# Three taps of VectorE's chains go to ScalarE and GpSimd, and a sampling's last six rounds are kept free

## The chip, the cores and the metric

The kernel runs on one NeuronCore of a Trainium2 chip. The metric is the device time of one execution in microseconds (us); lower is better. The profile names the engines PE (TensorE's matmuls), PEld (its weight loads), DVE (VectorE), ACT (ScalarE), POOL (GpSimd) and SP (the queue that issues most DMAs).

## The reference

Four images of 256 channels, 64x64 pixels, float32, go through four layers. Each is `x = x + layer(groupnorm(x))`.

```python
# layer 0: deformable convolution (DCN) and an MLP
y   = leaky_relu(bn(conv1x1(x)));  t = leaky_relu(bn(depthwise3x3(y)))
offset, mask = conv1x1(t), softmax(conv1x1(t))        # 4 groups x 9 points a pixel
d   = conv1x1(sum_points(mask * bilinear_sample(conv1x1(y), offset)))
x2  = bn(y + d);  x3 = x2 * sigmoid(se_up(relu(se_down(mean(x2)))))
out = y + fc2(leaky_relu(fc1(x3)))
# layer 1: linear attention with a second scale
qkv = relu(bn(conv1x1(x)));  agg = depthwise5x5(qkv) * w + b     # 768 channels, 25 taps
q, k, v = split(concat(qkv, agg));  out = relu(bn(proj((v k^T) relu(q) / sum)))
# layer 2: 3x3 convolution with binarised weights
# layer 3: non-local attention of 4096 positions over the 1024 of a 2x2 max pooling
```

## The kernel before

Channels lie on the 128 partitions, in two halves. The work on an image is written as Python generators that emit instructions and yield a cost after each piece:

- `sample(n)`: the bilinear sampling of image n, 288 rounds. A round (`gathered`) has four indirect DMAs, which GpSimd issues (L607) and which gather 128 rows into one of seven buffers `g`, and small matmuls that weigh and add them (L614). Eighteen rounds are a block; its sums are turned (L619, L624, L634), projected with `ow` (L647), added to y (L653) and stored as x2 (L661).
- `feedforward(n)`: squeeze and excitation and the MLP. It loads its weights f1, f2, sd, su (L704 to L710), takes the mean over x2, needs the excitation before it can scale f1 (L727), and then runs L752 and L762, 512 columns a matmul, over eight blocks.
- `layer1(n)`, called linear: `rows` makes qkv of a block (L837) and copies it into padded tiles; `aggregate` makes the 5x5 depthwise convolution of 128 channels x 16 rows as a chain of 25 instructions on VectorE (`depthwise`, L179; the first, with the bias, is L181), each `acc = pixels * tap + acc` on 1024 elements, with `acc` in PSUM (`agg`); the transposed keys and values are multiplied into `sums` (`outer`, L886 to L895); `output` divides and projects (L938 to L971). What is not a tap waits in a list `later` and is emitted one piece at a time by `step` between taps.
- `layer2(n)`: the 3x3 convolution in a Winograd form for two columns (matmul L1102). Its differences `xd` (L1053) are on VectorE, but on GpSimd when `alone`. `layer2_fours` (L1211) is a form for four columns, used for image 3.
- `layer3(n)`: the pooling attention. `first` takes the maxima (L1277, L1280), then four rounds a block of scores (L1315), maximum (L1316), exponential (L1321), transposes (L1327), copies (L1329), values (L1333), scaling (L1338), and the last product (L1343).

`beside(steps, number, *works)` sets the order by hand: each work has a total cost and a window of the share of steps, and after each step the works emit until their spent cost has caught up with the share. When a share has reached a work's end, what is left of the work is emitted at once. Inside `ordered()` the order of TensorE, VectorE, ScalarE and GpSimd is the order of emission; SP's order is the scheduler's own.

While image n is sampled, feedforward(n-1) runs in the share 0 to 0.22 (`FEED`), linear(n-1) in 0.22 to 1 (`LINEAR`), and the convolution and pooling of image n-2 in 0.22 to 1 (`SECOND`). Image 0 is sampled beside the first convolutions.

After the last sampling comes the tail, with `alone` set. Over 900 steps: feedforward(3) in 0 to 0.27, linear(3) in 0.27 to 1 (`LAST`), the convolution of image 2 in 0.27 to 0.53 (`CONV2`), its pooling in 0.53 to 1.02 (`POOLED`). Then `layer2_fours` of image 3, then its pooling. In the tail linear(3)'s 24 chains are shared: of three chains VectorE takes two and one (`aside`) is made by `products`: ScalarE multiplies each tap (L197, L199) into one of three tiles `m`, and GpSimd adds (L201). A step of `aside` is emitted at every second tap of VectorE's chains.

Of the kernel before, what the change touches and what calls it, by code (L numbers as in the profile page):

```python
# [9 lines left out]
F32 = mybir.dt.float32  # L10
I32 = mybir.dt.int32
AF = mybir.ActivationFunctionType
ALU = mybir.AluOpType
# [4 lines left out]
P = 128  # L18
N, C, H, W = 4, 256, 64, 64
# [4 lines left out]
G, PT = 4, 9  # L24
Q = G * PT
CT = 8
NCH = NT // CT
# [7 lines left out]
LEADS = 12, 14, 16, 18  # L35
# [37 lines left out]
class Net:  # L73
# [93 lines left out]
        at, n = ROWS[name]  # L167
        return self.rows[:, at:at + n]

    def depthwise(self, acc, src, w, k, rows, cols, r0, bias=None, step=lambda cost: cost, out=None):  # L170


        nc = self.nc
        for t in range(k * k):
            s = src[:, r0 + t // k:r0 + t // k + rows, t % k:t % k + cols]
            wt = w[:, t:t + 1]
            if t:
                to = acc if out is None or t < k * k - 1 else out
                nc.vector.scalar_tensor_tensor(to, s, wt, acc, ALU.mult, ALU.add)  # L179
# [7 lines left out]
    def products(self, pool, acc, src, w, k, rows, cols, r0, bias, step):  # L187

        nc = self.nc
        made = []  # L190
        for t in range(k * k + 3):
            if t < k * k:
                s = src[:, r0 + t // k:r0 + t // k + rows, t % k:t % k + cols]
                m = pool.tile([P, rows, cols], F32, name="m", tag="product", bufs=3) if t else acc
                made.append(m)
                if t:
                    nc.scalar.activation(m, s, AF.Copy, scale=w[:, t:t + 1])  # L197
                else:
                    nc.scalar.activation(m, s, AF.Identity, bias=bias, scale=w[:, t:t + 1])  # L199
            if 2 <= t <= k * k:  # L200
                nc.gpsimd.tensor_tensor(acc, acc, made[t - 1], ALU.add)  # L201
            yield step(0.5)


    def setup(self):
        nc, cp, a = self.nc, self.cp, self.a
# [3 lines left out]
        nc.sync.dma_start(self.cn, a["con"])  # L210
        self.rows = cp.tile([P, NROWS], F32, name="rows")
        nc.sync.dma_start(self.rows, a["rows"])
        self.ow = cp.tile([P, G, C], F32, name="ow")
        nc.sync.dma_start(self.ow, a["outproj_wT"])
        self.ident = cp.tile([P, P], F32, name="ident")
        make_identity(nc, self.ident)
        self.ones = cp.tile([P, P], F32, name="ones")
# [481 lines left out]
    def feedforward(self, n, ssum, st):  # L699
        nc, tc, a = self.nc, self.tc, self.a  # L700
        with tc.tile_pool(name=f"fa{n}", bufs=1, side="right") as sp, \
# [6 lines left out]
            nc.sync.dma_start(sd, a["se_down_wT"])  # L708
            su = sp.tile([64, C], F32, name="su")
            nc.sync.dma_start(su, a["se_up_wT"])  # L710
            mean = sp.tile([P, KT], F32, name="mean")
            nc.vector.tensor_reduce(mean, ssum, AX.X, ALU.add)
            nc.vector.tensor_scalar(mean, mean, 1.0 / HW, None, ALU.mult)
# [31 lines left out]
            for b in range(NB):  # L745
# [3 lines left out]
                for m in range(4 * KT):  # L749
# [3 lines left out]
                    t = bp.tile([P, 512], F32, name="lk")  # L753
# [16 lines left out]
    def layer1(self, n, st, st2):  # L770
        nc, tc, a = self.nc, self.tc, self.a
        rw = lambda v: v.rearrange("p (r w) -> p r w", w=W)
        fl = lambda v: v.rearrange("p r w -> p (r w)")
        with tc.tile_pool(name=f"la{n}", bufs=1, side="right") as sp, \
# [10 lines left out]
            ld = sp.tile([P, 4, 2, 32], F32, name="ld")  # L785
            nc.vector.memset(ld, 0.0)

            later, count, aside, every = [], 0, None, 2
            alone = self.alone
            room = lambda bufs, more=1: bufs + more * alone  # L790

            def step(cost, chains=False):


                nonlocal count
                count += chains
                if later and (not alone or count % every or not chains):
                    todo = later.pop(0)
                    todo()
                    cost += 0 if alone else getattr(todo, "cost", 0)  # L800
                if chains:
                    if count % 8 == 6 if alone else count in LEADS:
                        next(made, None)
                    if count % 2 and aside:
                        next(aside, None)
                return cost


# [46 lines left out]
                            if not alone:  # L855
                                yield

            def aggregate(pd, i, name, done, relu=True, **more):
# [3 lines left out]
                yield from self.depthwise(acc, pd, self.w5[:, i], 5, 16, W, 0, bias=self.b5[:, i:i + 1],  # L862
                                          step=lambda cost: step(cost, True), out=out)
# [62 lines left out]
            def output(c, qp, aq):  # L926

                nonlocal every
                every = 3
# [94 lines left out]
            while number < 6 * NCH:  # L1024
                count = 0 if not alone and number % 2 == 0 else count
                *args, more = yield from chain()
                if alone:

                    *slow, smore = yield from chain()
                    aside = products(*slow, **smore)  # L1030
                    yield from aggregate(*args, **more)
                    *args, more = yield from chain()
                    yield from aggregate(*args, **more)
                    for _ in aside:
                        pass
                    number += 3
                else:
                    yield from aggregate(*args, **more)
                    number += 1
            while later:  # L1040
                yield step(1.2 if alone else 1)

# [305 lines left out]
    def run(self):  # L1348
# [5 lines left out]
        feed = lambda n: self.feedforward(n, ssum[n], st[1][n % 2])  # L1354
# [5 lines left out]
        def second(n):  # L1360
            yield from conv(n)
            yield from pooled(n)
# [149 lines left out]
```

## Time and profile before

| | us |
|---|---|
| runs before: lowest, median, highest of 3 | 7437.45, 7441.21, 7445.19 |
| the profiled execution's own time | 7427.54 |
| its span, first to last instruction | 7425.7 |
| busy: PE, DVE, ACT, POOL | 5885.9, 4870.1, 3564.6, 4928.8 |
| first to last gather of images 0, 1, 2, 3 | 138 to 1598, to 3051, to 4504, to 5976 |
| feedforward(3)'s matmuls | 6032 to 6254 |
| linear(3) beside convolution(2) | 6268 to 6520 |
| linear(3) beside pooling(2), to its last tap | 6520 to 7008 |
| convolution(3), then pooling(3) | 7087 to 7214, to 7426 |

Mean granted clock of TensorE: 0.845. A row of a timeline reads: start, time, engine, line, operation, out<-in, shapes, how many in a row, and in brackets the idle time of the engine before it and what ended it. A row of waits reads: who waited for whom: us in all, times, the longest. A group's row ends in busy time and mean ns of one, and idle time before. In a table of stretches each engine's busy time stands with its count of instructions, then the granted clock, the share of DMA and GB/s. In the page's 40 slices each digit is the busy share in tenths of 185.6 us.

### The profile page before, as it was taken

Reading aid. Unit: us, or ns where it says so; the run is one execution under the profiler, and the core shown is the slowest. Engines: PE = TensorE matmul, PEld = TensorE weight load, DVE = VectorE, ACT = ScalarE, POOL = GpSimd, SP = SyncE. Lnnn points to the kernel's source line nnn. Section 1 sums busy time; section 2 is a strip of 40 time slices with the busy share of each in tenths; the row PEclk is TensorE's granted clock in tenths of the full one; section 3 lists DMA queues with packets and bytes.
Section 4 is the critical chain, followed back from the end, with each engine's and each line's share of the span. In section 5 each row is a group of like instructions: output and inputs, shape, how many; then the busy total and the mean of one; then the engine's idle time right before and its main releaser. Section 6 shows DMA issues by size and latency. Waiting matters only on the chain. (4 is left out here: it accounts for less than half of the span.)

```text
span 7425.7 us, 98944 instructions
## 1 busy us (share of the span) xinstructions
PE 5885.9 (79%) x35584; PEld 3436.3 (46%) x35584; DVE 4870.1 (66%) x6099; ACT 3564.6 (48%) x10807; POOL 4928.8 (66%) x4850
## 2 busy tenths in 40 slices
PE   5676766569777777898877788988777889977889
PEld 2333333334433333345655444456554444844477
DVE  6455552644488777326989883269998833999863
ACT  2444444445554444455556554554565532655425
POOL 1777777777777777777777776777777710865410
PEclk7776776779877767898988889989889899988899
DMA  6564654666544445555554445555544431210141
GB/s 187 148 191 144 176 173 137 174 183 190 178 127 125 125 125 147 168 156 167 159 155 139 141 147 187 153 167 159 156 142 145 146 115 65 81 54 34 49 124 49
DMA packets 743149, 1037.48 MB, mean 140 GB/s; under 512 B 352000, under 2 KB 457856, under 8 KB 741248
## 3 DMA queue, kind: packets, MB, share of 16 engines
q0 software_dynamic: 221184, 604.27, 27.8%
q1 hardware_dynamic: 521472, 426.87, 19.0%
q8 instruction: 280, 4.59, 0.3%
q14 instruction: 213, 1.74, 0.1%
HBM read 857.44 MB, written 173.33 MB: 139 GB/s over the span
## 5 line engine op out<-in xcount | busy, mean ns | idle before, releaser
L607 POOL DMA_INDIRECT g<-tab,sl x4608 | 4403.3, 956 | 1571.9 <-issue 1285.6
L179 DVE SCALAR_TENSOR_TENSOR agg<-pad,vec,agg 128x1024 f32<-128x1024 f32 x2280 | 2934.3, 1287 | 64.3
L599 ACT ACTIVATE wm<-sl,con 128x48 f32<-128x48 f32 x6144 | 1496.1, 363 | 24.9 <-DMA sl<-sd 11.8
L614 PE MATMUL dp<-g,wm 128*32 128x128 f32 x9216 | 664.2, 317 | 312.2 <-DMA g<-tab,sl 308.7
L614 PE MATMUL acc<-g,wm 128*32 128x128 f32 x9216 | 664.2, 318 | 298.5 <-DMA g<-tab,sl 285.5
L614 PEld LDWEIGHTS dp<-g,wm 128*32 128x32 f32 x9216 | 324.4, 119 | 664.4 <-DMA g<-tab,sl 493.4
L614 PEld LDWEIGHTS acc<-g,wm 128*32 128x32 f32 x9216 | 325.3, 120 | 661.4 <-DMA g<-tab,sl 452.5
L1102 PE MATMUL ps<-xd,w 128*128 128x256 f32 x2304 | 547.1, 386 | 47.9 <-ACT kt L891 38.6
L1102 PEld LDWEIGHTS ps<-xd,w 128*128 128x128 f32 x2304 | 430.5, 193 | 131.7 <-ACT kt L891 40.3
L752 PE MATMUL ps<-x2f,f 128*128 128x512 f32 x1024 | 479.0, 613 | 4.7 <-ACT f L727 4.0
L762 PE MATMUL ps<-hm,f 128*128 128x512 f32 x1024 | 467.7, 604 | 0.0
L837 PE MATMUL ps<-xr,qw 128*128 128x512 f32 x768 | 442.8, 706 | 31.2 <-DMA xr<-x 20.9
L737 DVE SCALAR_TENSOR_TENSOR hm<-ps,vec,lk 128x512 f32<-128x512 f32 x256 | 191.5, 751 | 372.8 <-ACT lk L754 369.2
L619 ACT COPY at<-dp 128x256 f32<-128x256 f32 x288 | 107.3, 373 | 679.9 <-PE dp L614 668.6
L619 ACT COPY at<-acc 128x256 f32<-128x256 f32 x288 | 107.2, 372 | 594.0 <-PE acc L614 584.0
L754 ACT ACTIVATE lk<-ps,low 128x512 f32<-128x512 f32 x256 | 175.7, 688 | 363.1 <-PE ps L752 359.2
L1333 PE MATMUL ps<-gt,pT 128*128 128x129 f32 x2048 | 303.3, 307 | 34.4 <-ACT pT L1329 32.2
L1333 PEld LDWEIGHTS ps<-gt,pT 128*128 128x128 f32 x2048 | 286.7, 219 | 87.5 <-ACT pT L1329 48.7
L647 PE MATMUL po<-dT,ow 128*128 128x288 f32 x1024 | 299.3, 440 | 25.5 <-ACT dT L642 11.6
L1315 PE MATMUL s<-ph,th 128*128 128x512 f32 x512 | 280.7, 659 | 44.9 <-DVE ot L955 13.8
L201 POOL TENSOR_TENSOR ak<-ak,m 128x1024 f32<-128x1024 f32 x96 | 229.0, 2385 | 119.3 <-ACT m L197 115.7
L201 POOL TENSOR_TENSOR av<-av,m 128x1024 f32<-128x1024 f32 x96 | 227.8, 2373 | 113.2 <-ACT m L197 109.2
(286 smaller groups left out, 8337.6 us busy)
## 6 DMA issues: line engine op xcount, KB each, us to landing
g<-tab,sl POOLq DMA_INDIRECT x4608
x<-x SPq DMA_DIRECT2D x112, 512.0 KB
xr<-x SPq DMA_DIRECT2D x96, 512.0 KB
tab<-xo SPq DMA_DIRECT2D x192, 128.0 KB
x<-in_x SPq DMA_DIRECT2D x32, 512.0 KB
y<-yc SPq DMA_DIRECT2D x32, 512.0 KB
yb<-y SPq DMA_DIRECT2D x64, 256.0 KB
x<-yb SPq DMA_DIRECT2D x64, 256.0 KB
```

Source lines behind the costliest of these rows:

```text
L179: nc.vector.scalar_tensor_tensor(to, s, wt, acc, ALU.mult, ALU.add)
L201: nc.gpsimd.tensor_tensor(acc, acc, made[t - 1], ALU.add)
L599: nc.scalar.activation(wm[:, :, :, o], blocks[b][:, r:r + WR, G:], AF.Copy, scale=self.con("own")[:, o:o + 1])
L607: nc.gpsimd.indirect_dma_start(out=g[:, i, :], out_offset=None, in_=table, in_offset=bass.IndirectOffsetOnAxis(ap=sl.bitcast(I32)[:, r, i: ...
L614: nc.tensor.matmul(acc[32 * i:32 * i + 32, :], wm[:, r4, 4 * i + 2 * x:4 * i + 2 * x + 2, :], g[:, i, x * P:(x + 1) * P], start=x == 0, st ...
L647: nc.tensor.matmul(po[m][:, 0:BR * OB], self.ow[:, k, m * P:(m + 1) * P], dT[b][:, k].rearrange("p r o -> p (r o)"), start=k == 0, stop=k ...
L752: nc.tensor.matmul(ps, f1[:, k, m * P:(m + 1) * P], x2[:, k], start=k == 0, stop=k == KT - 1)
L762: nc.tensor.matmul(ps, f2[:, k, m * P:(m + 1) * P], hm[:, k], start=k == 0, stop=k == 4 * KT - 1)
L837: nc.tensor.matmul(ps, qw[:, k, m * P:(m + 1) * P], x[:, k], start=k == 0, stop=k == KT - 1)
L1102: nc.tensor.matmul(ps[:, e], w[:, k, t, 2 * half + e, m * P:(m + 1) * P], v[:, 2 * half + e, k, t:t + 8], start=i % 6 == 0, stop=i % 6 == 5)
L1315: nc.tensor.matmul(s[i], tv[:, 4 * b + j], ph[:, i * 512:(i + 1) * 512], start=True, stop=True)
L1333: nc.tensor.matmul(ps[:, 0:P + 1], pT[:, m], gt[:, m], start=m == 0, stop=m == 7)
```

## The change

There are four edits.

1. Windows beside a sampling end at 0.98 of its 288 rounds (`END`) where they ended at 1. A new work, `(feeds[n + 1], 1, END, 2)`, emits the first piece of the next feedforward in round 283: `feedforward` now yields once after its four weight loads, and the generators are made once, in `feeds`.
2. `ow` moves from the constants to the samplings' own pool, so that its 4 KB a partition are free in the tail.
3. In the tail VectorE's 16 chains begin at tap 3 (`LEAD`). `begun` makes the first three taps with `products`: ScalarE's three products, GpSimd's two additions, into a tile `lead` in SBUF, which VectorE's first tap reads in the place of `acc`. From the eighth tap of a chain on (`FETCH`) the next chain is asked for, and at every odd tap after that a step of its lead is emitted.
4. Paces follow: `LAST` 582 to 514, the convolution's window in the tail 0.27 to 0.57 and the pooling's 0.57 to 1.02, `aside` at two of three taps, pieces of `later` at four, then five of seven taps where it was one of two, then two of three, rows at one tap in seven where it was one in eight.

```diff
-LINEAR, LAST = 956, 582
-STEPS, BEGUN = 900, 0.22
+LINEAR, LAST = 956, 514
+STEPS, BEGUN, END = 900, 0.22, 0.98
+LEAD, FETCH = 3, 8
+TAPS, SKIP = 25 - LEAD, ((1, 3, 5, 6), (0, 1, 3, 4, 6))
...
-        for t in range(k * k):
+        for t in range(begun, k * k):
...
-                nc.vector.scalar_tensor_tensor(to, s, wt, acc, ALU.mult, ALU.add)
+                nc.vector.scalar_tensor_tensor(to, s, wt, acc if t > begun else lead, ALU.mult, ALU.add)
...
-        self.ow = cp.tile([P, G, C], F32, name="ow")
-        nc.sync.dma_start(self.ow, a["outproj_wT"])
...
             nc.sync.dma_start(su, a["se_up_wT"])
+            yield 1
...
-                if later and (not alone or count % every or not chains):
+                if later and (not alone or not chains or count % 7 in SKIP[every]):
...
-                    if count % 8 == 6 if alone else count in LEADS:
+                    if count % 7 == 5 if alone else count in LEADS:
                         next(made, None)
-                    if count % 2 and aside:
+                    at = count % TAPS
+                    if aside and (2 * at) % 3 < 2:
                         next(aside, None)
+                    if wanted and at >= FETCH:
+                        fetched()
+                    if ahead and at % 2:
+                        next(ahead, None)
...
+            def begun(pd, i, *_):
+                made = []
+                def taps():
+                    made.append(bp.tile([P, 16, W], F32, name="lead", bufs=1))
+                    yield from self.products(bp, made[0], pd, self.w5[:, i], 5, 16, W, 0, self.b5[:, i:i + 1], lambda cost: cost, LEAD)
+                return made, taps()
...
+            if alone:
+                wanted = True
+                for i in range(4 * NCH):
+                    (*args, more), mine = yield from first()
+                    ahead = None
+                    if not i % 2:
+                        *slow, smore = yield from chain()
+                        aside = products(*slow, **smore)
+                    wanted = i + 1 < 4 * NCH
+                    yield from aggregate(*args, lead=mine, **more)
+                    if i % 2:
+                        for _ in aside:
+                            pass
...
-        behind = lambda n: [(feed(n), FEED, 0, BEGUN), (linear(n), LINEAR, BEGUN, 1)]
+        behind = lambda n: [(feeds[n], FEED, 0, BEGUN), (linear(n), LINEAR, BEGUN, END), (feeds[n + 1], 1, END, 2)]
...
+            self.ow = self.sp.tile([P, G, C], F32, name="ow", bufs=1)
+            self.nc.sync.dma_start(self.ow, self.a["outproj_wT"])
...
-                    beside(self.sample(n, ssum[n]), rounds, *behind(n - 1), (second(n - 2), SECOND, BEGUN, 1))
+                    beside(self.sample(n, ssum[n]), rounds, *behind(n - 1), (second(n - 2), SECOND, BEGUN, END))
...
-            beside(range(STEPS), STEPS, (feed(N - 1), FEED, 0, 0.27), (linear(N - 1), LAST, 0.27, 1), (conv(N - 2), CONV2, 0.27, 0.53), (rest, POOLED, 0.53, 1.02))
+            beside(range(STEPS), STEPS, (feeds[N - 1], FEED, 0, 0.27), (linear(N - 1), LAST, 0.27, 1), (conv(N - 2), CONV2, 0.27, 0.57), (rest, POOLED, 0.57, 1.02))
```

More of the change, by code (lines that the diff above doesn't have):

```diff
@@ L168, in row, with depthwise @@
         return self.rows[:, at:at + n]
-    def depthwise(self, acc, src, w, k, rows, cols, r0, bias=None, step=lambda cost: cost, out=None):
+    def depthwise(self, acc, src, w, k, rows, cols, r0, bias=None, step=lambda cost: cost, out=None, begun=0, lead=None):
         nc = self.nc
-        for t in range(k * k):
+        for t in range(begun, k * k):
             s = src[:, r0 + t // k:r0 + t // k + rows, t % k:t % k + cols]
@@ L185, in depthwise, with products @@
                 yield step(1.3 if self.alone else 3.9)
-    def products(self, pool, acc, src, w, k, rows, cols, r0, bias, step):
+    def products(self, pool, acc, src, w, k, rows, cols, r0, bias, step, taps=None):
         nc = self.nc
-        made = []
-        for t in range(k * k + 3):
-            if t < k * k:
+        made, taps = [], taps or k * k
+        for t in range(taps + 3):
+            if t < taps:
                 s = src[:, r0 + t // k:r0 + t // k + rows, t % k:t % k + cols]
@@ L199, in products @@
                     nc.scalar.activation(m, s, AF.Identity, bias=bias, scale=w[:, t:t + 1])
-            if 2 <= t <= k * k:
+            if 2 <= t <= taps:
                 nc.gpsimd.tensor_tensor(acc, acc, made[t - 1], ALU.add)
@@ L786, in layer1 @@
             nc.vector.memset(ld, 0.0)
-            later, count, aside, every = [], 0, None, 2
+            later, count, aside, ahead, every = [], 0, None, None, 0
+            then, lead, wanted = None, None, False
             alone = self.alone
@@ L856, in rows, with aggregate @@
                                 yield
-            def aggregate(pd, i, name, done, relu=True, **more):
+            def aggregate(pd, i, name, done, relu=True, lead=None, **more):
                 acc = self.ps1.tile([P, 16, W], F32, name="agg", tag="agg")
@@ L862, in aggregate @@
                 yield from self.depthwise(acc, pd, self.w5[:, i], 5, 16, W, 0, bias=self.b5[:, i:i + 1],
-                                          step=lambda cost: step(cost, True), out=out)
+                                          step=lambda cost: step(cost, True), out=out, begun=LEAD * alone, lead=lead and lead[0])
                 end(out, done, relu, **more)
+            def begun(pd, i, *_):
[4 more added lines that the diff above has]
+                return made, taps()
             def products(pd, i, name, done, relu=True, **more):
@@ L928, in output @@
                 nonlocal every
-                every = 3
+                every = 1
                 qh = [[q[:, 2 + 8 * h:10 + 8 * h, 2:W + 2] for q in qp] + [v[:, 8 * h:8 * h + 8, :] for v in aq] for h in range(2)]
@@ L1022, in chain, with fetched, first @@
                 return args
-            while number < 6 * NCH:
-                count = 0 if not alone and number % 2 == 0 else count
-                *args, more = yield from chain()
[L1027 to L1039, printed above, removed]
+            def fetched():
+                nonlocal then, lead, ahead, wanted
+                then = next(them)
+                if then:
+                    wanted = False
+                    lead, ahead = begun(*then)
+            def first():
+                while wanted:
+                    fetched()
+                    yield step(0.5)
+                for _ in ahead or ():
+                    yield step(0.5)
+                return then, lead
+            if alone:
[11 more added lines that the diff above has]
+                            pass
+            while not alone and number < 6 * NCH:
+                count = 0 if number % 2 == 0 else count
+                *args, more = yield from chain()
+                yield from aggregate(*args, **more)
+                number += 1
             while later:
@@ L1352, in run @@
         st = {i: [tile(f"st{i}{n}", [P, KT, NB, 6]) for n in range(2)] for i in (1, 2, 3)}
-        feed = lambda n: self.feedforward(n, ssum[n], st[1][n % 2])
+        feeds = [self.feedforward(n, ssum[n], st[1][n % 2]) for n in range(N)]
         linear = lambda n: self.layer1(n, st[1][n % 2], st[2][n % 2])
```

## The prediction

> **What bounds the kernel now.** I read the page's 40 slices first, then the gathers of GpSimd, then a table of stretches over the tail, then who waits for whom in each stretch.
>
> ```profile
> DVE  6455552644488777326989883269998833999863
> POOL 1777777777777777777777776777777710865410
> ```
>
> GpSimd is flat at 7 from slice 2 on: those are the gathers, 0.95 us busy and 0.30 us of issue each, 1.25 us apart, 1152 for one image. Each image takes 1452 to 1472 us from its first gather to its last, so four samplings fill 138 to 5976 us, and everything else there is free as long as it does not hold a gather. From slice 34 on (the tail, 5976 to 7426 us) no gathers are left and VectorE stands at 9. So the change works in two places: at the ends of samplings, and in the tail.
>
> End of a sampling, around the last gather of image 3: the timelines of GpSimd, of TensorE and of the SP queue.
>
> ```profile
> 5975.51 0.95 POOL L607 DMA_INDIRECT g<-tab,sl  x1 [0.30 <-issue]
> ```
>
> ```profile
> 6005.57 0.65 PE L614 MATMUL dp<-g,wm 128*32 128x128 f32 x16
> 6006.15 3.70 PE L960 MATMUL ps<-ot,pw 128*128 128x512 f32 x8
> 6010.98 1.98 PE L1343 MATMUL ps<-m,ww 128*128 128x512 f32 x4 [1.13 <-ACT m L1338]
> ...
> 6027.79 0.56 PE L716 MATMUL ps<-mean,sd 128*64 128x1 f32 x4 [9.18 <-DMA su<-in_se_up_wT]
> ```
>
> ```profile
> 6018.56 0.36 SPq L704 DMA_DIRECT2D f<-in_fc_wT  x1
> ```
>
> The last gather ends at 5976.5, its matmul at 6006.2: TensorE runs 30 us behind, with linear and pooling work of earlier images (L960, L1343) between. Then 25 us pass before feedforward's first L752 at 6031.5, 7.7 us of it on weights that SP only asks for at 6018.6. In all 55.0 us in which nothing but leftovers runs. One image earlier the same lag reaches the gathers (GpSimd's waits, 4504 to 4600 us):
>
> ```profile
> POOL g L607 <- PE acc L614: 15.2, 2, 13.6
> POOL g L607 <- DMA xyf<-x: 6.0, 1, 6.0
> ```
>
> Tail: busy time in five stretches (PE, PEld, DVE, ACT, POOL, then clock and DMA).
>
> ```profile
> 6268.00:6520.00 252.00, 248.73 (x1168) 198.85 (x1168) 219.92 (x261) 152.38 (x216) 200.84 (x101) 0.98 0.26 74
> 6520.00:7008.00 488.00, 356.75 (x1379) 225.10 (x1380) 450.59 (x522) 279.74 (x398) 294.96 (x124) 0.83 0.13 44
> ```
>
> 6268 to 6520 is linear beside the 3x3 convolution of image 2: TensorE is busy 248.7 of 252, so **TensorE** bounds it; VectorE (220) and GpSimd (201) have some air. 6520 to 7008 is linear beside pooling: VectorE is busy 450.6 of 488 and **VectorE** bounds it. So the taps taken from VectorE pay in the second stretch, not in the first.
>
> **The change, part by part.**
>
> *Six free rounds.* 0.98 of 288 rounds: linear and the convolution/pooling work now end in round 283, and the order of instructions has nothing but gathers, their matmuls and four weight loads in the rounds after it. Six rounds are 24 gathers, 30 us, in which TensorE works off its lag; its own part of a round is some 1.1 us (0.65 for L614, 0.2 for L624, 4.15 / 18 for L647). Three terms:
>
> A. The waits at 4523 to 4575 us (13.6 + 6.0 + 1.6 + 1.2, less 0.3 of normal issue each) go: -21 us.
>
> B. The same work stands in 0.76 of the rounds where it had 0.78, 2.6% denser. In the samplings of images 2 and 3 a round's matmul ends 12 to 31 us behind its last gather, and seven g buffers of 5.0 us a round, less the round itself, allow about 30; the peaks already touch that (3.4 us of GpSimd wait once in image 2, 2.6 us in image 3). Bounds: 0, if the rest of the lag is free, and 29 us an image, if the whole shift comes back. In both images the lag climbs from 12 to 30 us in the middle, over some 125 us, and from 13 to 30 towards the end, over some 180; 2.6% of these stretches is 3.3 and 4.7, and I take that 8 us for each image: +16 us. Images 0 and 1 lag under 20 us: 0.
>
> C. The 55.0 us at the end become some 8 us of lag plus the chain from the last matmul to L752: 25.3 as measured, less 7.7 of weight wait and some 3 of L960/L1343: 15. So 23: -32 us. Bounds -22 (lag stays at 18) and -40 (no lag). The loads of f1, f2, sd, su pass from the start of feedforward to before it; in SP's order the sl loads of the next image stand ahead of them, so a gather cannot queue behind their wait; what does is the last x2 store, which waits for VectorE anyway. At image 3 the conv weights (w2) now load behind feedforward's first blocks; they are wanted 240 us later, nothing.
>
> *Three taps of 16 chains.* VectorE loses 16 x 3 = 48 taps. A tap is 1285 ns by its row, 1.325 us from start to start:
>
> ```profile
> L179 DVE SCALAR_TENSOR_TENSOR agg<-pad,vec,agg 128x1024 f32<-128x1024 f32 x368 | 472.9, 1285 | 8.6
> L201 POOL TENSOR_TENSOR ak<-ak,m 128x1024 f32<-128x1024 f32 x96 | 229.0, 2385 | 119.3 <-ACT m L197 115.7
> L197 ACT ACTIVATE m<-pad,vec 128x1024 f32<-128x1024 f32 x192 | 219.4, 1160 | 3.6 <-POOL av L201 3.6
> ```
>
> 48 x 1.325 = 64 us off VectorE; ScalarE gets 48 products x 1.16-1.24 = 57 us, GpSimd 32 additions x 2.38 = 76 us. In the order the lead of a chain is finished 5 to 8 taps (7 to 10 us) before the tap that reads it, except for the first chain, whose first tap comes some 7 us later; TensorE covers that.
>
> D. Convolution stretch. The pace is set again (0.27 to 0.57, and the products go at 2/3 of the steps): by the new order it holds 143 taps (before 140), 91 chain additions on GpSimd (66), and on TensorE 8 more 512-column matmuls, 28 transposes and 10 sums, 16 x 0.43 + 28 x 0.107 + 20 x 0.107 = 12 us. TensorE: 252 + 12 = 264. GpSimd: 91 x 2.38 + 32 x 1.27 = 257, and it can't start before 6268 nor add before about 6287. Three engines are now within a few per cent, and TensorE waits for GpSimd's xd additions, which stand in one queue with the chain's. Lower bound 264 (TensorE alone), upper 264 + 14 pairs of xd x three queued products x 2.38 = 364. GpSimd's 257 and its 19 us of idle start make 276; with a few waits I take 285: +33 us.
>
> E. Pooling stretch. 208 taps instead of 259: 51 x 1.325 = -68 us. Against it: the first tap of each chain now reads pad and lead, both in SBUF, where it read a constant or PSUM. This trace has such a pair: the maximum L1277, normally 0.68 us, while GpSimd adds:
>
> ```profile
> 6546.58 2.35 POOL L201 TENSOR_TENSOR ak<-ak,m 128x1024 f32<-128x1024 f32 x1 [3.57 <-ACT m L197]
> 6546.80 2.67 DVE L1277 TENSOR_TENSOR m<-x 128x512 f32<-128x512 f32 x1
> ```
>
> It ends 0.5 us after GpSimd does. The 16 such instructions (L1277, L1280) of this stretch lost 10 us together, 0.63 each with GpSimd busy 60% of the time; at 75% that is 0.8, for 9.5 chains +8. And VectorE, no longer far behind, will wait more for TensorE's scores (27 us of such gaps now): +10. Sum -50 us, between -35 and -68. TensorE (357 less the 12 moved, of 438) and GpSimd (133 x 2.38 = 317) stay below.
>
> The Trainium skill, SBUF — State Buffer (the section on the two physically separate sides), gives the rule behind this row: VectorE and GpSimd share one pair of ports as an exclusive lock, which an operation with two SBUF inputs holds or waits for a whole instruction long. Read at its worst, every first tap would wait a whole addition, 9.5 x 2.38 = 23 us for the 8 above, and the sum below would be 15 us less of a gain; the row's 0.63 us on average, 2.0 at most, says less, and I go by the row.
>
> The Trainium skill, GPSIMD Engine Reference (introduction and Key points), speaks against the change as such: GpSimd is the wrong engine for elementwise arithmetic, VectorE being about twice as fast. If GpSimd's 76 us counted against VectorE's 64 everywhere, D and E would be +12 together and the sum -23; the rows have GpSimd idle for 190 of the second stretch's 488 us, so there its price is not on the path.
>
> F. After linear's last tap some pooling pieces more are left (40 matmuls L1333 for 32, 36 transposes for 32) in a latency chain: +2 us. The lead tile takes the place of ow in SBUF; ow's load moves behind three others at the start: 0.
>
> Sum: -21 + 16 - 32 + 33 - 50 + 2 = **-52 us**. The profiled execution took 7427.5 us, which becomes 7375.5; it lies 13.7 us below the median of the runs, 7441.2, so in runs I expect 7389.
>
> **The rivals.**
>
> 1. *More gain.* TensorE alone bounds D (+12), no new gather waits (B 0), holds as priced: -21 - 32 + 12 - 60 + 2 = -99: 7342. For it: TensorE's waits for xd are 4.3 us in all today. Against: GpSimd's 257 us of work in 264.
>
> 2. *The samplings give it back.* TensorE and VectorE (88 to 90% busy in images 2 and 3) can't take 2.6% more per round: B is 58, sum -10: 7431, no change. Against it: the lag falls back to 12 us again and again.
>
> 3. *Slower: GpSimd starves the convolution.* Every pair of xd additions finds three queued products: D +112, sum -52 - 33 + 112 = +27: 7468. It decides from D = +85 up, some 5 us a pair. Against it: ScalarE feeds GpSimd and is itself held by TensorE, so queues of three should be rare.
>
> 4. *The taps buy nothing*: D and E cancel, only A, B, C, F stay: -35, 7406. That the order has the 48 taps out is seen in it, so the change does what it says.
>
> **How the numbers follow.** Forecast 0.45, rival 1 0.20, rival 4 0.11, rival 2 0.12, rival 3 0.12. About 0.2% (15 us) is what can be told from no change: 7426 to 7456. Faster: forecast, 1, 4 and a little of 2, 0.77; same 0.11; slower 0.12. Range: the ends of the terms, -21 + 0 - 40 + 12 - 68 + 0 = -117 and -21 + 32 - 22 + 50 - 35 + 4 = +8, give 7324 to 7449; rival 2 is inside. I leave out the upper end's last 10 us: 7325 to 7439.
>
> **What would show it.** Right: gathers without a wait over 2 us after 4504; 20 to 27 us from the last gather to L752's counterpart; convolution stretch 275 to 295 us, with waits of the conv matmul on xd of 10 to 30 us; pooling stretch 425 to 450; first taps of 1.3 to 3.5 us beside GpSimd's additions. Wrong: gather waits over 30 us in images 2 and 3 together, a convolution stretch over 330 or at 264, or a pooling stretch over 465.

## The result, and the profile after

The changed kernel is **slower** by 1.7%: 7569.1 us, median of 5 runs (7561.5 to 7575.2), against 7439.8 for the kernel before beside it, a ratio of 1.0174 with a 95% interval of 1.0159 to 1.0189. The forecast was 7389 in a range of 7325 to 7439. The time lies outside, on the other side.

The page's rows of VectorE and GpSimd after (a slice is 189.0 us; the span is 7559.4 us, the execution's own time 7561.5):

```profile
DVE  6454452644588787228988872289887824888763
...
POOL 2777777777777777777776667777766612976410
```

GpSimd's row is no longer flat: it falls to 6 in slices 22 to 24 and 30 to 32. These are the second halves of the samplings of images 2 and 3. Its waits in image 2's second half, first before, then after:

```profile
POOL g L607 <- PE dp L614: 6.7, 9, 3.4
POOL g L607 <- PE acc L614: 3.2, 7, 1.0
```

```profile
POOL g L607 <- PE acc L614: 41.4, 18, 9.9
POOL g L607 <- PE dp L614: 36.8, 18, 8.5
```

GpSimd waits until TensorE's matmul frees a g buffer. Over the normal 0.30 us of issue, the gathers of images 2 and 3 wait 67.3 and 71.6 us; before it was 4.9 and 24.5. The last gather ends at 6085.0, 108.5 us later than before.

The transition to feedforward did become short, as a timeline of GpSimd and one of TensorE show:

```profile
6084.08 0.94 POOL L607 DMA_INDIRECT g<-tab,sl  x1 [0.30 <-issue]
```

```profile
6108.44 3.78 PE L753 MATMUL ps<-x2f,f 128*128 128x512 f32 x4 [1.75 <-ACT f L728]
```

23.4 us instead of 55.0. (After, L753 and L763 are before's L752 and L762; tap L181, products L199 and L201, additions L203, 3x3 convolution L1138, xd L1089.) The tail, convolution stretch and pooling stretch:

```profile
6344.50:6652.00 307.50, 272.84 (x1229) 211.50 (x1230) 229.38 (x267) 198.76 (x267) 260.24 (x124) 0.95 0.23 63
6652.00:7130.00 478.00, 354.92 (x1303) 217.48 (x1301) 399.76 (x466) 288.01 (x394) 316.37 (x133) 0.82 0.13 42
```

In the first, TensorE is no longer full (273 of 307.5 us). In the second VectorE's busy time fell by 53 us against before, but the stretch by only 12. Bounded by the same events in both traces:

| stretch | before | after | change | predicted |
|---|---|---|---|---|
| to the last gather | 5976.5 | 6085.0 | +108.5 | -21 + 16 (A, B) |
| last gather to feedforward | 55.0 | 23.4 | -31.6 | -32 (C) |
| convolution stretch | 249.5 | 307.2 | +58 | +33 (D) |
| pooling stretch, to the last tap | 490 | 478 | -12 | -50 (E) |
| last tap to the end | 418 | 430 | +12 | +2 (F) |

The rows add up to +135, the spans differ by 133.7. So about 77 us are lost in samplings and transition, and 57 from feedforward's first matmul to the end (1394 to 1451).

In some sessions of measuring, called long sessions below, the kernel before itself took 8513 to 8575 us; one kernel, begun24, was traced in both kinds, with a span of 8623 us there and 7480 otherwise, and its gathers waited 1224 us there and 80 otherwise, which is the whole difference. Times from a long session are compared only with before beside them; of their traces only the tail is set beside others, because begun24's feedforward (222 us) and its two stretches (249 and 489) came out there as in the kernel before.

### The profile page after: what moved, and what is told of

Read it like the earlier page. It is cut to its first block, busy times and chain, and to the rows that moved or that the text cites. A ratio compares the mean times of both kernels' runs of the same rounds, so it can differ in the third digit from the quotient of the medians.

```text
span 7559.4 us, 98990 instructions
## 1 busy us (share of the span) xinstructions
PE 5896.9 (78%) x35584; PEld 3433.2 (45%) x35584; DVE 4829.7 (64%) x6051; ACT 3620.5 (48%) x10855; POOL 5009.5 (66%) x4882
## 4 chain that ended last, share of the span: by engine, by line
PE 31%; DVE 17%; POOL 12%; issue 8%; ACT 6%; DMA 5%; SPq 0%; POOLq 0%; DVEq 0%; ACTq 0%
DVE agg L181 11%; POOL g L607 9%; PE ps L753 5%; PE ps L763 4%; DMA g<-tab,sl 3%; PE ps L1369 2%; PE ps L977 2%; PE s L1351 2%; PE ps L844 2%; PE ps L1247 2%; ACT wm L599 2%; PE po L647 1%; POOL av L203 1%; PE ps L1138 1%; PE dp L614 1%
## 5 line engine op out<-in xcount | busy, mean ns | idle before, releaser
L181 DVE SCALAR_TENSOR_TENSOR agg<-pad,vec,agg 128x1024 f32<-128x1024 f32 x2232 | 2872.6, 1287 | 62.9
L614 PE MATMUL acc<-g,wm 128*32 128x128 f32 x9216 | 636.5, 313 | 292.8 <-DMA g<-tab,sl 280.1
L1138 PE MATMUL ps<-xd,w 128*128 128x256 f32 x2304 | 548.4, 387 | 7.7 <-POOL xd L1089 4.3
L844 PE MATMUL ps<-xr,qw 128*128 128x512 f32 x768 | 465.6, 738 | 58.7 <-DMA xr<-x 21.9
L753 PE MATMUL ps<-x2f,f 128*128 128x512 f32 x1024 | 479.6, 614 | 6.0 <-DMA x2f<-x 3.1
L1138 PEld LDWEIGHTS ps<-xd,w 128*128 128x128 f32 x2304 | 433.1, 194 | 90.1 <-issue 32.6
L763 PE MATMUL ps<-hm,f 128*128 128x512 f32 x1024 | 466.1, 602 | 0.0
L1369 PE MATMUL ps<-gt,pT 128*128 128x129 f32 x2048 | 308.5, 309 | 72.3 <-ACT pT L1365 70.3
L647 PE MATMUL po<-dT,ow 128*128 128x288 f32 x1024 | 322.2, 466 | 35.2 <-DVE x L1122 16.2
L1369 PEld LDWEIGHTS ps<-gt,pT 128*128 128x128 f32 x2048 | 287.7, 219 | 133.7 <-ACT pT L1365 91.5
L203 POOL TENSOR_TENSOR ak<-ak,m 128x1024 f32<-128x1024 f32 x96 | 231.4, 2411 | 96.2 <-ACT m L199 91.9
L753 PEld LDWEIGHTS ps<-x2f,f 128*128 128x128 f32 x1024 | 189.1, 193 | 226.0 <-issue 210.2
```

The lines of the kernel that those rows point to most:

```text
L181: nc.vector.scalar_tensor_tensor(to, s, wt, acc if t > begun else lead, ALU.mult, ALU.add)
L614: nc.tensor.matmul(acc[32 * i:32 * i + 32, :], wm[:, r4, 4 * i + 2 * x:4 * i + 2 * x + 2, :], g[:, i, x * P:(x + 1) * P], start=x == 0, st ...
L647: nc.tensor.matmul(po[m][:, 0:BR * OB], self.ow[:, k, m * P:(m + 1) * P], dT[b][:, k].rearrange("p r o -> p (r o)"), start=k == 0, stop=k ...
L753: nc.tensor.matmul(ps, f1[:, k, m * P:(m + 1) * P], x2[:, k], start=k == 0, stop=k == KT - 1)
L763: nc.tensor.matmul(ps, f2[:, k, m * P:(m + 1) * P], hm[:, k], start=k == 0, stop=k == 4 * KT - 1)
L844: nc.tensor.matmul(ps, qw[:, k, m * P:(m + 1) * P], x[:, k], start=k == 0, stop=k == KT - 1)
```

## The experiments

**The two halves alone.** *taps_only* is the changed kernel with windows to 1 and no early weights; *free_only* is the kernel before with the free rounds and the weights.

```diff
 # taps_only, from after
-        behind = lambda n: [(feeds[n], FEED, 0, BEGUN), (linear(n), LINEAR, BEGUN, END), (feeds[n + 1], 1, END, 2)]
+        behind = lambda n: [(feeds[n], FEED, 0, BEGUN), (linear(n), LINEAR, BEGUN, 1)]
...
-(second(n - 2), SECOND, BEGUN, END))
+(second(n - 2), SECOND, BEGUN, 1))
```

> The change with the windows beside the samplings ending at 1 again and no weight load ahead; the tail's leads and paces stay. Theory S (the samplings lost the time: their gathers waited 67 and 72 us where they had waited 5 and 25) and theory T (the tail, from feedforward(3)'s first matmul to the end, lost 57 us by itself: 1394 to 1451) are parted here. S and T as measured in the two profiles: gather waits of images 2 and 3 back at 5 and 25 us, 55 us from the last gather to L753, tail from there 1451: 7440 + 57 = 7497. Rival (the leads cost nothing by themselves, the tail is late through what the samplings leave): 7440.

Measured: 7491.2, ratio 1.0069 [1.0053, 1.0086]. Gather waits 5.6 and 25.2 us as before; feedforward's first matmul to the end 1452.

```diff
-STEPS, BEGUN = 900, 0.22                 # free_only, from before
+STEPS, BEGUN, END = 900, 0.22, 0.98
...
+            yield 1
...
-        behind = lambda n: [(feed(n), FEED, 0, BEGUN), (linear(n), LINEAR, BEGUN, 1)]
+        behind = lambda n: [(feeds[n], FEED, 0, BEGUN), (linear(n), LINEAR, BEGUN, END), (feeds[n + 1], 1, END, 2)]
...
-(second(n - 2), SECOND, BEGUN, 1))
+(second(n - 2), SECOND, BEGUN, END))
```

> The kernel before with the six free rounds and the weight loads ahead alone; the tail as it was, ow among the constants. If the samplings lose by themselves: gather waits of 67 and 72 us in images 2 and 3, 23 us from the last gather to feedforward(3), tail after it 1394: 7440 + 62 + 47 - 32 = 7517. Rival (the place of ow in SBUF, or the pool it moved to, makes the waits): the waits stay at 5 us, 21 us go at image 3's start, 32 at its end: 7387.

Measured: 7515.7, ratio 1.0105 [1.0088, 1.0122]; waits 72.1 and 73.3 us, gather to feedforward 17.5, tail 1400 for before's 1394. +52 and +76 make the changed kernel's +129: the two losses add up. `ow` keeps its place here, so its move is not the cause.

**Is it VectorE's load in the samplings?**

```diff
+            if k == 5 and t == 12 and not self.alone:
+                continue
```

> free_only with one of the 25 taps of each 5x5 chain beside a sampling left out (24 chains an image, 32 us of VectorE; the output lacks that tap). Theory D (density: 2.6% more work a round is more than VectorE's order can take in the second half of a sampling): 32 us is as much as the six rounds took away, so the gather waits fall from about 70 us an image to under 25, and the time to under 7430. Rival P (the new places of the pieces, not their amount: a few coincidences of a long wait): the waits stay over 50 us an image, 7500 or more.

Leaving out one of 25 taps takes some 32 us of VectorE from every image's sampling. Measured: 7499.2, ratio 1.0083 [1.0063, 1.0103], waits 62.9 and 68.7. Only 14 of 145 us went. VectorE's amount of work is not what binds. The amounts of work of TensorE and ScalarE were not varied alone.

**The same free rounds at the old density.** The windows start earlier, at 0.20, and are 0.78 wide again.

```diff
-STEPS, BEGUN, END = 900, 0.22, 0.98
+STEPS, BEGUN, END = 900, 0.2, 0.98
```

> free_only with the windows of linear and of the convolution beginning at 0.20, not 0.22, so that they are as wide as before (0.78); feedforward has 290 us for matmuls that keep TensorE busy for 220 beside the sampling. D: the waits in the second half of the samplings go back to 5 us, and new waits of 10 to 40 us stand in the first fifth, where TensorE is 94% busy already. P: the waits of the second half stay near 70 us.

Measured: **7378.4**, one run, with 7439.2 before beside it. Waits 0.9 and 7.3 us; last gather at 5957.0, feedforward 20.4 us later. GpSimd's waits in image 2's second half:

```profile
POOL g L607 <- PE acc L614: 2.4, 8, 0.3
POOL g L607 <- PE dp L614: 2.1, 7, 0.3
```

The long waits on TensorE are gone, and -21 (A) and -32 (C) are earned without giving anything back in the samplings. The profiled execution of before was 12 us under the median of its runs; from trace to trace the gain is 49 us, not 61. drop3 and lead1 below, which are other kernels with the same windows, confirm the samplings: their gathers of images 2 and 3 wait 8 and 7 us together and end at 5959.6 and 5958.0. Timed again, in a long session:

> The kernel before with six free rounds, feedforward's weights loaded there, and BEGUN 0.20: timed for an interval. All theories: 7365 to 7390, 0.990 to 0.993 of before.

8530.2 against 8574.7, ratio 0.9945 [0.9932, 0.9959]. It is faster than both kernels. The gain is smaller there, 44 us for 61.

**Density or place?** *begun24* is before with windows from 0.24 to 1, 0.76 wide at other rounds; *second_to_1* is free_only with the convolution/pooling window open to 1 again.

```diff
-STEPS, BEGUN = 900, 0.22                 # begun24, from before
+STEPS, BEGUN = 900, 0.24
```

```diff
-(second(n - 2), SECOND, BEGUN, END))     # second_to_1, from free_only
+(second(n - 2), SECOND, BEGUN, 1))
```

Both met a long session first and told nothing on this question (begun24 1.0064 [1.0044, 1.0084], second_to_1 0.9988 [0.9974, 1.0002]). Their expectations were repeated, and so they are shown once:

> The kernel before with BEGUN 0.24 for 0.22 and windows that end at 1 (0.76 of the rounds, no free rounds), on a chip with the clock of the first runs. Theory T (density): gathers of images 2 and 3 wait 50 to 75 us each, gather to feedforward 45 to 60 us, 7530 to 7570. Rival P (place): waits of both images together under 40 us, 7435 to 7455.

Measured: 7481.4, ratio 1.0057 [1.0034, 1.0079]; waits 28.3 and 48.4.

> free_only, but the convolution/pooling work may use a sampling's rounds up to the last again (0.78 of them), linear ends at 0.98 (0.76); on a chip with the clock of the first runs (the run called second_to_1 had a clock of 0.80 through the samplings, where TensorE holds the gathers of every image). Theory T1 (it is the density of the pooling work's hand-offs that holds TensorE's queue): gather waits of images 2 and 3 fall from 145 to under 40 us together, 7400 to 7430. Rival T2 (linear's density, TensorE's amount of work and VectorE's taps): waits stay at 110 to 150, 7490 to 7520.

Measured: 7448.6, ratio 1.0015 [1.0003, 1.0026]; waits 32.7 and 37.7.

Both lie between the theories. A width of 0.76 costs waits at other rounds too, 77 us for before's 29, but half of what free_only's place costs (145). Giving only the convolution/pooling work its old density takes 75 of free_only's 145 us away; of the 70 left, the 41 above before's 29 stay with linear's narrower window alone. The lag of TensorE, measured from the end of a round's last gather to the end of that round's matmuls, taken at every twelfth round, shows how little room there is. From the middle of image 2's sampling to share 0.92 of its time it lies at 4 to 18 us in free_begun20, 12 to 31 before, 18 to 33 in second_to_1, and 22 to 37 in the changed kernel. The prediction put the room of the seven buffers at about 30. TensorE itself is not full there: 210 of 300 us from 3900 to 4200. Among its waits those for ScalarE are the longest; image 2's second half, from 3600 us on, first before, then after, then free_begun20 (850, 920 and 850 us):

```profile
PE pt L1327 <- ACT pe L1321: 24.8, 14, 3.6
PE acc L624 <- ACT at L619: 21.9, 11, 9.1
...
PE ps L1333 <- ACT pT L1329: 8.6, 14, 1.3
```

```profile
PE pt L1363 <- ACT pe L1357: 41.3, 19, 9.4
PE acc L624 <- ACT at L619: 34.8, 13, 8.7
PE ps L1369 <- ACT pT L1365: 23.0, 19, 5.8
```

```profile
PE pt L1328 <- ACT pe L1322: 33.7, 17, 8.4
...
PE ps L1334 <- ACT pT L1330: 15.3, 14, 4.1
PE acc L624 <- ACT at L619: 12.5, 8, 2.7
```

These three rose from 55 to 99 us. But free_begun20 has 62 us of them, more than before, and hardly a gather waits there; so these waits alone do not tell why the lag stays. The next kernel spaced two of these hand-offs, the exponentials and the copies of the transposes, by a round.

```diff
-yield 1.5 ... 2 ... 1 ... 1 ... 1.5 ... 1.5     # pooling's paces, in order
+yield 1.4 ... 2.6 ... 0.5 ... 2.6 ... 1 ... 0.9
```

> free_only with the seven paces inside a pooling group set anew at the same sum (1.5, 2, 1, 1, 1, 1.5, 1.5 to 1.4, 2.6, 0.5, 0.5, 2.6, 1, 0.9): in the order the transposes of the exponentials now always come a round or more after the exponentials, and the sums a round or more after the copies of the transposes (in free_only 7 and 21 of 32 stood in one round). Same work, same windows. Theory H1 (TensorE stands still for ScalarE's part of the pooling, handed over too close before): gather waits of images 2 and 3 fall from 145 to under 60 us together, 7390 to 7440. Rival H2 (it is the number of hand-offs per round, whichever pair stands close): 110 to 160 us, 7490 to 7530.

It was run three times (*handoff*, *handoff_b*, *handoff_c*), each time in a long session, where images 2 and 3 waited 306 to 351 us each: 8622.0 (ratio 1.0054 [1.0036, 1.0073]), 8552.1 (1.0046 [1.0032, 1.006]) and 8533.4 (8515.2 before). H1 and H2 are not told apart. Only the tail speaks: its pooling stretch was 503, 507 and 507 us instead of 490, so there these paces cost 13 to 17 us.

> free_begun20 with the paces of handoff. Theory H1: no gather waits to lose in the samplings; in the tail's pooling stretch, where VectorE's taps set the time, little to gain: 7360 to 7380. Rival H2 (the pairs now pushed together, transposes with their copies and sums with reciprocals, cost as much or more): 7385 to 7430.

8556.3, ratio 0.997 [0.9957, 0.9984] in the session where free_begun20_b had 0.9945. The paces lose; in the tail (1415 us from feedforward to the end, 1396 in free_begun20_b) H2's side holds.

**The tail: whose work costs what?** All from the changed kernel with BEGUN 0.20.

> The whole change with BEGUN 0.20 for 0.22: six rounds are free, and linear and the convolution/pooling work have 0.78 of the rounds as before. The samplings and the step to feedforward should be as in free_begun20 (last gather at 5950 to 5965, 20 us to feedforward), and the tail as in the changed kernel. Theory T with its tail (three taps from ScalarE and GpSimd cost 57 us from feedforward's first matmul to the end, 1394 to 1451): 7378 + 57 = 7435, between 7420 and 7450. Rival: the tail's loss came from something left over by the samplings and goes with it: 7320 to 7385.

It met a long session: 8589.9, ratio 1.0014 [1.0005, 1.0024], and a second run of it (*after_begun20_b*) 8588.8, 1.0019 [1.0009, 1.0029]. The tail is 1451 and 1457 with the old density in the samplings, for 1452 in taps_only and 1451 in the changed kernel: its loss is its own. (All tails here run from feedforward's first matmul to the end of the span, as in the table; the 1448 of the next expectation is 3 us low by this.) The total of 7420 to 7445 outside a long session was not seen.

*drop3*: the three taps are made by nobody.

```diff
-LINEAR, LAST = 956, 514
+LINEAR, LAST = 956, 512
...
-            if t:
+            if t > begun or lead is not None:
...
-                    made.append(bp.tile([P, 16, W], F32, name="lead", bufs=1))
-                    yield from self.products(bp, made[0], pd, self.w5[:, i], 5, 16, W, 0, self.b5[:, i:i + 1], lambda cost: cost, LEAD)
+                    made.append(None)
+                    yield 0
```

> after_begun20 with the first three taps of the 16 chains left out altogether: VectorE makes 22 taps a chain as in the changed kernel, ScalarE's 48 products and GpSimd's 32 additions for them are not done (three taps of linear are missing from the output). Only the tail is read (from feedforward's first matmul: convolution stretch, pooling stretch to the last tap, end; 1394 us in the kernel before, 249.5 and 490 of it; 1448 here with the taps on ScalarE and GpSimd). Theory V (VectorE's taps set the pooling stretch; the loss comes from what ScalarE and GpSimd are given): convolution 250 to 265, pooling 420 to 445, 1330 to 1355 to the end. Rival H (in the pooling stretch the hand-offs between TensorE, ScalarE and VectorE are already the limit, and taps ride in their gaps): convolution 250 to 265, pooling 465 to 490, 1375 to 1400.

Its two stretches:

```profile
6214.50:6485.00 270.50, 261.31 (x1226) 206.39 (x1227) 225.16 (x269) 175.58 (x248) 224.01 (x111) 0.98 0.26 73
6485.00:6926.00 441.00, 334.36 (x1307) 204.99 (x1305) 385.85 (x464) 258.73 (x366) 270.83 (x114) 0.87 0.14 46
```

Pooling 440: V holds there, some 51 taps fewer are worth 50 us. But the convolution takes 270 even without the leads (+21), outside both ranges, the end 434 (+16), and 1380 to the end lies in H's range, not in V's: free taps would have gained 14 us. The work on ScalarE and GpSimd then costs 1451 - 1380 = 71 us (38 beside the convolution, 34 beside pooling), so the tail loses 57. The time was 7361.0, one run, with 7438.5 before beside it.

*lead1*: ScalarE makes one tap a chain, GpSimd adds nothing for it, rows at before's pace.

```diff
-LINEAR, LAST = 956, 514
+LINEAR, LAST = 956, 555
-LEAD, FETCH = 3, 8
+LEAD, FETCH = 1, 8
-                    if count % 7 == 5 if alone else count in LEADS:
+                    if count % 8 == 6 if alone else count in LEADS:
```

> after_begun20 with one tap per chain (the first, with the bias) made ahead by ScalarE and none added by GpSimd; the other 24 on VectorE; whole-row products at the pace of before. Only the tail is read. Theory G (GpSimd's queue beside the convolution, with the additions of the leads in it, made that stretch 58 us longer): convolution stretch 250 to 270 us. Rival A (ScalarE's part does it: products of the leads stand ahead of the rows' copies, or the first chain waits for its lead): over 285. For the pooling stretch, theory V says 490 - 10 x 1.33 = 475 or less, rival H 485 to 495 (no gain).

Convolution 285, just on A's side; pooling 466, V's side; 1409 to the end; 7389.0, one run, with 7438.5 before beside it. Without one addition for the leads the convolution still takes 15 us more than in drop3; as it also holds 157 of VectorE's taps where drop3 has 145, the 15 are not ScalarE's alone.

*leads_late*: three taps ahead only from the seventh chain on, rows at before's pace (`% 8 == 6` as above), and the convolution's window ending at 0.55.

```diff
-LINEAR, LAST = 956, 514
+LINEAR, LAST = 956, 543
...
-out=out, begun=LEAD * alone, lead=lead and lead[0])
+out=out, begun=LEAD if lead else 0, lead=lead and lead[0])
...
-                    lead, ahead = begun(*then)
+                    late += 1
+                    lead, ahead = begun(*then) if late > 6 else (None, None)
```

> after_begun20 with the first three taps made by ScalarE and GpSimd only from the seventh of the 16 chains on, that is in the pooling stretch (10 chains, 30 taps), the whole-row products at the pace of before, and the convolution's window ending at 0.55. Theory K (the first taps cost time only beside the convolution, where GpSimd and ScalarE were full and the first chain waits for its lead; beside pooling VectorE still gains by them): convolution stretch 245 to 270 us, feedforward's first matmul to the end 1360 to 1394, time 7345 to 7380. Rival L (beside pooling the waits for TensorE and ScalarE are what binds, and a tap less on VectorE buys nothing or costs): convolution stretch as said, but 1394 to 1425 to the end, time 7380 to 7410.

Convolution 267, as both theories said, but pooling 505 and 1440 to the end, worse than both ranges; the ratio is 1.0007 [0.9997, 1.0017]. Beside pooling, three taps by three engines do not pay either. Two waits of VectorE there, before first, then drop3, then the changed kernel (leads_late has 33.1 and 20.9 us, like the latter):

```profile
DVE rden L1336 <- PE ps L1333: 8.0, 5, 2.6
...
DVE mx L1316 <- PE s L1315: 3.3, 13, 0.8
```

```profile
DVE mx L1352 <- PE s L1351: 23.4, 20, 4.7
DVE rden L1372 <- PE ps L1369: 8.4, 7, 2.7
```

```profile
DVE rden L1372 <- PE ps L1369: 33.8, 14, 5.5
DVE mx L1352 <- PE s L1351: 21.5, 23, 3.7
```

With the leads in ScalarE's queue the values (L1369) come late: +25 us of VectorE's waits, of the 38 by which after's pooling stretch is longer than drop3's. That they are late because ScalarE's copies of the transposes stand behind its products is argued from the order, not shown: TensorE's own waits for these copies are 21.1 us in after and 21.0 in drop3.

## Why the prediction was wrong

**A (-21), right.** free_begun20 ends its gathers 19.5 us earlier.

**B (+16), the step that failed most.** It came to some +130 (-21 + 130 = +109). I priced 2.6% more density as 2.6% of the stretches in which the lag climbs. Each climb was taken to fall back to 12 us afterwards, as it does in before. In the changed kernel it does not: from the middle of the image to share 0.92 the lag at the rounds taken never falls under 22 us and rises to 37, about the room of the seven buffers, so that a further delay becomes a wait of the gathers. Even the upper bound, 29 us an image, took the shift of the work for the most that could come back, and the range used only 32 of these 58. Rival 2 named the place, but its price (58) was under half, and its reason, VectorE's and TensorE's full load, does not hold: for VectorE it fell with free_24taps, and TensorE's 88 to 90% holds in before only up to 3671 us: in the two stretches of 300 us from there to 4271 it was busy 225 and 236 us. That narrower windows raise the waits is shown at two places, and that windows of the old width take them away is shown with the same six rounds free; why 0.22 to 0.98 leads to 145 us of waits and 0.24 to 1 to 77, and whether the close hand-offs to ScalarE are the mechanism, stays open.

**C (-32), right in size**, by the chain as priced: 23.4 us.

**D (+33), mis-sized: +58.** I named the engine and missed the chain. Of the 58, TensorE is busy 26 us more (273 for 247) and idle 32 us more. GpSimd's additions were to be felt by the convolution's wait for xd, and that wait stayed at 4.3 us in after. TensorE waits for ScalarE instead, as after's waits in this stretch show:

```profile
PE pt L904 <- ACT v L852: 10.8, 4, 6.6
PE vk L912 <- ACT kt L908: 9.3, 6, 2.3
PE ps L844 <- ACT kt L908: 5.9, 4, 4.1
PE ps L1138 <- POOL xd L1089: 4.3, 1, 4.3
```

In before the v and kt waits of this stretch were 0.5 us together. ScalarE in turn waits for GpSimd to free a product tile, after first, then drop3:

```profile
ACT m L199 <- POOL av L203: 38.2, 26, 3.6
...
ACT m L199 <- POOL ak L203: 18.3, 14, 2.8
ACT m L199 <- POOL lead L203: 6.8, 7, 1.2
```

```profile
ACT m L199 <- POOL av L203: 23.5, 19, 3.6
...
ACT m L199 <- POOL ak L203: 6.5, 6, 1.6
```

63 us against 30, and before 3.6. ScalarE works in the order of emission, so what stands behind a product, such as the copies that TensorE needs, waits with it; in drop3 TensorE's waits for v and kt are 7 us, for 29 in after. Rival 3 had GpSimd starving TensorE, by the wrong path. The first chain is late too: its first tap starts 38.1 us after the first xd, not 14.9. The chain's own waits:

```profile
6375.43 1.24 ACT L201 ACTIVATE lead<-pad,b,vec 128x1024 f32<-128x1024 f32 x1
...
6377.80 4.81 POOL L203 TENSOR_TENSOR lead<-lead,m 128x1024 f32<-128x1024 f32 x2 [19.91 <-ACT m L199]
...
6382.64 3.37 DVE L181 SCALAR_TENSOR_TENSOR agg<-pad,vec,lead 128x1024 f32<-128x1024 f32 x1 [18.27 <-POOL lead L203]
```

The lead's first product stands behind the rows' copies in ScalarE's queue, and VectorE idles 18.3 us for it. GpSimd's 19.9 us are not new: it waits 19.2 us for its first product in before, too. That "TensorE covers that" was wrong is not shown: in the stretch's first 39.5 us TensorE is busy 36.7, before 37.9 of 39.7, and its added idle time lies later, where GpSimd is the fullest engine:

```profile
6344.50:6384.00 39.50, 36.74 (x147) 25.29 (x148) 2.53 (x12) 24.08 (x41) 13.55 (x9) 0.92 0.27 73
6384.00:6652.00 268.00, 236.10 (x1084) 186.22 (x1083) 226.85 (x256) 174.68 (x227) 246.69 (x116) 0.96 0.22 62
```

So GpSimd's work was priced right (260 us for 257); what was too small are its waits around it, 28 us (19 of idle start and "a few waits") for the 47 of the trace. drop3 shows the rest: the extra TensorE work, priced at 12 us, is some 14 (261 busy for 247), and makes most of its +21.

**E (-50), half right.** The taps' worth was right: in drop3 VectorE is busy 67 us less in this stretch, for the 68 priced. The step that failed is the +10 for VectorE's waits: its idle time, 37 us before, is 78 after, +41. In drop3, without leads, it is 55, +18; that drop3's stretch is shorter by just the 50 of E is luck, since the +8 for held first taps is not in it. The hold of a first tap was right on average: the 16 first taps that read `lead` took 1.27 to 3.47 us, 12.4 us over the normal 1.29 together, 0.78 each for the 0.8 priced; but the nine in this stretch lost 4 us, for the 8 of the sum. The Trainium skill, SBUF — State Buffer (the section on the two separate sides), says that VectorE and GpSimd share ports under an exclusive lock; the long first taps agree with that, but seven of the 16 took no longer than 1.32 us, so the price is not a whole addition each.

**F (+2), +12.** With fewer taps to ride on, more of the projection and pooling is left behind the last tap; drop3 has 434 us there, after 430, so the leads are not the cause.

The Trainium skill, GPSIMD Engine Reference (introduction), has GpSimd as the wrong engine for elementwise work. Priced that way D and E were +12 together; measured is +46. GpSimd's own time is a part of that, as it was busy 247 of the last 268 us beside the convolution; the queues that wait for each other are the rest, and no run parts the two.

## What to carry to other kernels

When a queue already touches its cap, price a denser schedule by what happens when it stays there, not by the percentage; keep the density by moving the other end of the window too, which here turned +76 into -61 us (one run; 44 us, with an interval, in a long session). Before work is given to an engine "with air", list what stands behind it in that engine's in-order queue and who waits for that: a third engine may be the one that pays. To see what a transferred operation is worth and what it costs, leave it out altogether once: the difference to before is its worth, the difference to the change its price.

## What the runs showed of the hardware

I had not expected sessions that differ by 15%. It is not shown to be the chip: the record gives the number 14 to a session with before at 7438 us and, twenty minutes later, to one at 8513. In the long sessions the mean granted clock was 0.80 where it is 0.845 otherwise, and I first read that as the cause ("where TensorE holds the gathers", in an expectation above). The traces do not show it: from 500 to 1500 us TensorE was busy 488 us in begun24's long session (672 in before), and most of the gathers' extra wait there ended on a releaser that the profile does not name (`remote`). GpSimd's waits in that stretch:

```profile
POOL g L607 <- remote: 135.7, 61, 3.5
POOL g L607 <- PE dp L614: 11.9, 1, 11.9
```

What it is stays open. In the tail, with no gathers, begun24 kept before's two stretches within 1 us and their granted clocks (0.99 for 0.98, and 0.83), and after_begun20 those of the changed kernel within 4 us.
